# First layer of a small transformer stack: projecting the first block one sequence at a time, and the second block's projection among the first score rounds

## The chip, the cores and the metric

One Trainium2 chip, one of its cores. The metric is the device time of one launch in microseconds (us). The engines are named as in the profile: PE is TensorE's matmul, PEld its weight load, DVE is VectorE, ACT is ScalarE, POOL is GpSimd, SP is SyncE, which only issues transfers here. A q behind a name (SPq, ACTq) is that engine's sequencer, which issues DMAs.

## What is computed

The input is 16 sequences of 256 tokens with 128 channels. Four residual layers follow one another: causal attention with 16 heads of 8 channels (layer a), a mixture of 8 experts of which each token takes 2, attention without a mask with its own scaling (layer b), and the same mixture again. Cut to what matters here:

```python
x = x + attn_a(layernorm(x), wq, bq, wk, bk, wv, bv, wo, bo)   # causal, 16 heads of 8
x = x + ffn(layernorm(x), Wr, Wg, Wu, Wd)                      # top 2 of 8 experts
x = x + attn_b(layernorm(x), W_qkv, b_qkv, W_proj, b_proj)     # no mask, own scaling
x = x + ffn(layernorm(x), Wr, Wg, Wu, Wd)
```

The change is in layer a alone, in its first steps.

## The kernel before

The tokens are taken in 8 blocks of 512, that is of two sequences each; a block is held as four tiles of 128 tokens. For each block `project` computes the norms and the three projections. Its steps are: load the block; the moments (two DVE instructions for each tile, then POOL makes `rstd` and, where ScalarE is to norm, `shift`); the normed tiles `xn`; the four transposes of `xn` by PE and the copy `xnT` by ACT; k (matmul, bias on ACT, split into `hi` and `lo` by ACT and POOL); `lay` of k; q in the same way; `lay` of q; then v. `lay` spreads k or q over partitions so that every pair of heads has a row group of its own: four DMAs of 128 KB for one sequence, two from `hi` and two from `lo`, into one of four slots `ks[i]`, `qs[i]`. `project` is a generator: each `yield` gives the number of rounds until its next step and that step's load on VectorE, ScalarE and the one spare PSUM bank `mm`.

The attention itself runs in rounds. A round takes two pairs of heads of a sequence: 8 rounds make a sequence, 16 a block, 128 the layer. In round `at`, PE first computes the scores of that round with queries on the rows (`rows_scores`, tile `s<-k,q`), DVE takes their maxima (`rows_maxima`, tile `mx`), and 14 rounds later the scores are computed again, with the maxima folded in, for the exponentials on ACT. So rounds 0 to 7 read the first sequence's slots, 8 to 15 the second's, and round 16 is the first one of block 1.

All other work hangs on the rounds. `later(n, kind, steps, rank)` puts a generator on a list; `due`, called twice in each round, takes one step of every generator whose time has come, lowest rank first, as far as a budget for VectorE, ScalarE and the bank allows (rank -1 ignores the budget). Each engine takes its instructions in the order in which the Python emits them, so a matmul that waits holds back all of PE that is emitted behind it, and the same holds for each DMA queue.

Before the first round, the kernel before runs block 0's `project` for both sequences up to q, and block 1's `project` up to the transposes of its normed tiles:

```python
                second = project(1)
                next(second)
                while start() is not None:
                    pass
                later(2, work(s=0.7, bank=True), start.of, 0)
                later_constants()
...
                for i in range(2, RING):
                    later(0, FREE, prepared(i), 0)

                for _ in range(3):
                    step = next(second)
                later(*step, second, 0)
```

`prepared(i)` sets a slot's k and q tiles to zero on POOL (for slots 2 and 3) and lays rows of ones into it. In both layers `normed` (VectorE) is used for blocks 0 and 1, `normed_in_steps` (ScalarE) for later ones.

Of the kernel before, what the change touches and what calls it, by code (L numbers as in the profile page):

```python
# [41 lines left out]
F32 = mybir.dt.float32  # L42
# [4 lines left out]
ALU = mybir.AluOpType  # L47
# [16 lines left out]
NT = TB // P  # L64
# [14 lines left out]
def work(v=0.0, s=0.0, bank=False):  # L79

    return bank, v, s


FREE = work()
# [4 lines left out]
def layers(  # L89
# [21 lines left out]
    nc = tc.nc  # L111
    xt = x.flatten_outer_dims().rearrange("(n t p) d -> n p t d", t=NT, p=P)
# [49 lines left out]
    tables = ctx.enter_context(tc.tile_pool(name="tables", bufs=1))  # L162
    psum = ctx.enter_context(tc.tile_pool(name="mm", bufs=1, space=PSUM))
    x_first = blocks.tile([P, NT, P], F32, tag="xb")
    nc.sync.dma_start(out=x_first, in_=xt[0])
    queue = nc.scalar
    weights_a = attention_weights(
        wq_a, bq_a, wk_a, bk_a, wv_a, bv_a, wo_a, bo_a, 1.0 / math.sqrt(HD), "a"
# [59 lines left out]
    vs = [const.tile([P, NT, NH, 1 + HD], F32, name=f"v{i}") for i in range(3)]  # L228

    qs = [const.tile([P, NP, SEQ], F32R, name=f"q{i}") for i in range(RING)]  # L230
    ks = [const.tile([P, NP, SEQ], F32R, name=f"k{i}") for i in range(RING)]
# [3 lines left out]
    class InOrder:  # L235
# [78 lines left out]

    def moments(pool, xb, whole=False, ts=range(NT)):

        mv = pool.tile([P, NT, 2], F32, tag="mv")
        for t in ts:
            if t == NT // 2 and not whole:
                yield 1, work(0.9)  # L320
            st = pool.tile([P, nc.vector.BN_STATS_DIM], F32, tag="st", bufs=4)
            ve.bn_stats(st, xb[:, t, :])
            ve.bn_aggr(mv[:, t, :], st)
        rstd = pool.tile([P, NT], F32, tag="rstd")
        some = slice(ts[0], ts[-1] + 1)
        po.tensor_scalar_add(rstd[:, some], mv[:, some, 1], EPS)
        po.tensor_tensor(rstd[:, some], rstd[:, some], minus_half[:, some], ALU.pow)

        shift = pool.tile([P, NT], F32, tag="shift")
        if not whole:  # L330
            po.tensor_scalar_mul(shift, mv[:, :, 0], -1.0)
            po.tensor_tensor(shift, shift, rstd, ALU.mult)
        return mv, rstd, shift

    def normed_in_steps(xn, xb, rstd, shift):
        for t in range(NT):
            if t == NT // 2:
                yield 1, work(s=0.8)
            se.activation(
                xn[:, t, :], xb[:, t, :], AF.Identity,  # L340
                bias=shift[:, t : t + 1], scale=rstd[:, t : t + 1],
            )

    def normed(xn, xb, mv, rstd, ts):
        for t in ts:
            ve.tensor_scalar(
                xn[:, t, :], xb[:, t, :], mv[:, t, 0:1], rstd[:, t : t + 1],
                ALU.subtract, ALU.mult,
            )
# [463 lines left out]
    def attention(w, causal, name, mixture, ahead=None):  # L813

        with ExitStack() as own:
            pool = own.enter_context(tc.tile_pool(name=f"att_{name}", bufs=2))
# [28 lines left out]
            def project(n, b0=0, nb=2):  # L845
# [4 lines left out]
                xb, ts = xs[n], range(2 * b0, 2 * (b0 + nb))  # L850
# [3 lines left out]
                if not causal:  # L854
                    po.tensor_tensor(xb[:, ts[0] : ts[-1] + 1], xb[:, ts[0] : ts[-1] + 1], more, ALU.add)
                    yield 1, work(0.9)
                mv, rstd, shift = yield from moments(pool, xb, n < 2, ts)
                yield 3 if causal else 2, work(s=0.8)
                if causal and n == 0:
                    w["arrange"](ve)  # L860
                xn = pool.tile([P, NT, P], F32, tag="xn", bufs=1)
                if n < 2:
                    normed(xn, xb, mv, rstd, ts)
                else:
                    yield from normed_in_steps(xn, xb, rstd, shift)
                yield 2, work(s=0.6, bank=True)
                xnT = turned_block(pool, mm[0], xn, ts)

# [49 lines left out]
                for t in ts:  # L918
                    te.matmul(
                        pv[:, t, :], lhsT=xnT[:, bass.ts(t, P)], rhs=w["wv"],  # L920
                        start=True, stop=True,
# [6 lines left out]
                        :, ts[0] * NH : (ts[-1] + 1) * NH, :  # L928
                    ],
                )  # L930
                if causal and n == 0:

                    yield 1, FREE
                    yield from output_bias(w, pool, psum, name)
                while "extra" not in w:
                    yield 1, FREE
                some = xb[:, ts[0] : ts[-1] + 1, :]
# [291 lines left out]
            def later(rounds_on, kind, task, rank=1):  # L1229
                tasks.append((at + rounds_on, kind, rank, task))  # L1230

            def due(place):
                nonlocal taken
                over = at >= len(rounds)
                if place == 0:
                    taken = [0.0, 0.0]
                banks = 1
                for task in sorted((t for t in tasks if t[0] <= at), key=lambda t: (t[2], t[0])):
                    since, (bank, *times), rank, steps = task
                    more = 3.0 if over else 1.0 + 0.2 * (at - since)  # L1240
                    if rank >= 0 and (bank and not banks or any(
                        t and had and had + t > most * more
                        for t, had, most in zip(times, taken, room)
                    )):
                        continue
                    banks -= bank
                    taken = [had + t for had, t in zip(taken, times)]
                    tasks.remove(task)
                    then = next(steps, None)
                    if rank < 0 and then is not None and then[0] < 3:  # L1250

                        then = next(steps, None)
                    if then is not None:
                        later(then[0] if rank >= 0 or then[0] > 2 else 0, then[1], steps, rank)

            def fill():

                for _ in zeros():
                    yield 6, FREE

            if not causal:
                starts = [Steps(project(0, b, 1)) for b in range(2)]
                yield starts
# [6 lines left out]
            av = psum_v.tile([P, 2, SEQ], F32, tag="av")  # L1270
            ve.memset(av, 0.0)
            if causal:
                start = Steps(project(0))
                start()
                start()
                for i in range(2):
                    po.memset(ks[i].bitcast(F32), 0.0)
                start()
                for i in range(2):
                    ve.memset(qs[i].bitcast(F32), 0.0)  # L1280
                mask()
                for i in range(2):
                    for _ in prepared(i):
                        pass
                    po.memset(vs[i][:, :, :, 0], 1.0)
                po.memset(vs[2][:, :, :, 0], 1.0)
                second = project(1)
                next(second)
                while start() is not None:
                    pass  # L1290
                later(2, work(s=0.7, bank=True), start.of, 0)
                later_constants()
                later(16, FREE, fill())
                later(32, FREE, second_weights(pool, psum))
                for i in range(2, RING):
                    later(0, FREE, prepared(i), 0)

                for _ in range(3):
                    step = next(second)
                later(*step, second, 0)  # L1300
            else:
                begun, other = starts
                while not begun.ready:
                    begun()
                if not other.steps:
                    other()
                second = project(1)
                next(second)
                later(2, work(s=0.7, bank=True), begun.of, 0)
                later(0, FREE, chain(other.of, second), -1)  # L1310
            for n in range(2, NB):
                later((n - 1) * each - (9 if causal else 15), FREE, project(n), 0)
            while at < len(rounds) + lag + 4 or tasks or mixture.now:
                if at < len(rounds):
                    n, b, f, i = rounds[at]
# [3 lines left out]
                    s = rows_scores(n, b, 2 * f + i)  # L1319
# [53 lines left out]
    second = attention(weights_b, False, "b", following, mixture)  # L1373
    first, other = next(second)
# [59 lines left out]
```

## Time and profile before

| | us |
|---|---|
| median of three runs | 1261.02 (1259.92 to 1266.01) |
| the profiled execution | 1241.97 |
| its span (first to last instruction of the program) | 1239.7 |
| first score matmul (round 0) starts at | 35.27 |
| round 8 (second sequence) starts at | 47.90 |
| round 14 (first exponentials) starts at | 57.00 |
| round 16 (block 1) starts at | 62.09 |
| PE busy in the span | 1023.6 (83%) |

The starts of rounds are those of the groups `s<-k,q` on PE in the timeline, counted from the first. Times in the timeline run from the span's start. Nearly every row carries the line L245, that of the helper through which the kernel issues its instructions, so rows are told apart by their tiles: `k<-hi` is a DMA of `lay`, `xn<-xb,mv,rstd` a norm on VectorE, `xn<-xb,shift,rstd` a norm on ScalarE, `ps<-ident,xn` a transpose, `mx<-s` the maxima of a round. A bracket behind a row gives the engine's idle time ahead of it and what ended that.

### The profile page before, as it was taken

To read this page: it belongs to the slowest core of one execution; us is meant where nothing else is said; L and a number is where in the kernel's file an instruction comes from. 1 tells how busy PE (TensorE), PEld (TensorE's weight loads), DVE (VectorE), ACT (ScalarE), POOL (GpSimd) and SP (SyncE) were. 2 spreads that over 40 slices of the span, in tenths; PEclk is the share of its full clock that TensorE was granted. 3 is DMA by queue.
4 is the path that set the end of the run, shared out by engine and by line. 5 is a ranking of instruction groups with operands and counts; after the bars stand their busy time and mean duration, and the time that the engine had idled before them with its cause. 6 is when DMAs were issued, how large, how long until landed. Compare 5 with 4: busy or idle time off the path is not lost. (4 is left out here: it accounts for less than half of the span.)

```text
span 1239.7 us, 24231 instructions
## 1 busy us (share of the span) xinstructions
PE 1023.6 (83%) x8170; PEld 748.3 (60%) x8170; DVE 819.2 (66%) x2264; ACT 634.3 (51%) x1323; POOL 617.2 (50%) x687
## 2 busy tenths in 40 slices
PE   1798989878998999996577787768878888999991
PEld 0455555555776889985344444435546667799991
DVE  5666777876865766665577767667677536766662
ACT  1266666545554434453256676565746674444440
POOL 5344577555477785565221212332335675765551
PEclk9999999989999999999568899797979999999996
DMA  4334442425344698775232222222243436787866
GB/s 96 84 93 135 130 125 77 121 63 154 87 108 119 171 221 197 175 192 112 67 87 71 57 74 66 75 82 66 78 119 88 117 95 151 183 207 188 203 145 212
DMA packets 186478, 151.61 MB, mean 122 GB/s; under 512 B 16370, under 2 KB 161268, under 8 KB 186356
## 3 DMA queue, kind: packets, MB, share of 16 engines
q1 hardware_dynamic: 154754, 125.81, 36.0%
q0 software_dynamic: 26560, 18.76, 10.1%
q10 hardware_dynamic: 5042, 5.51, 1.5%
q8 instruction: 65, 1.06, 0.4%
q14 instruction: 57, 0.47, 0.1%
HBM read 82.74 MB, written 32.54 MB: 93 GB/s over the span
## 5 line engine op out<-in xcount | busy, mean ns | idle before, releaser
L245 DVE TENSOR_REDUCE mx<-s 128x6 f32<-128x768 f32 (+1 forms) x256 | 277.4, 1088 | 91.3 <-PE s L245 86.5
L245 ACT ACTIVATE p<-s 128x768 f32<-128x768 f32 (+1 forms) x256 | 234.8, 917 | 184.8 <-PE s L245 181.8
L245 POOL DMA_INDIRECT total<-y,to x156 | 244.0, 1564 | 138.9 <-ACT sg L245 80.5
L245 DVE SCALAR_TENSOR_TENSOR sg<-sg,gu 128x256 f32<-128x256 f32 x265 | 111.3, 420 | 144.5 <-ACT sg L245 108.5
L245 POOL DMA_INDIRECT rows_in<-both_rows,slots x128 | 127.5, 996 | 99.4 <-DVE both_rows L245 46.9
L245 PE MATMUL gu<-xT,w_g 128*128 128x256 f32 x530 | 162.4, 388 | 17.2 <-DVE sg L245 8.7
L245 PEld LDWEIGHTS y<-w_d,h 128*128 128x128 f32 x1248 | 165.0, 193 | 17.2 <-ACT y L245 4.8
L245 PE MATMUL y<-w_d,h 128*128 128x128 f32 x1248 | 167.4, 277 | 6.8 <-ACT y L245 3.7
L245 ACT ACTIVATE sg<-gu 128x256 f32<-128x256 f32 x265 | 101.7, 384 | 138.6 <-PE gu L245 87.1
L245 PE MATMUL gu<-xT,w_u 128*128 128x256 f32 x530 | 158.1, 380 | 0.0
L245 POOL TENSOR_SCALAR_AFFINE_SELECT p<-p 128x512 f32<-128x512 f32 x128 | 88.6, 698 | 107.6 <-ACT p L245 107.1
L245 PE MATMUL s<-k,q 62*128 62x256 f32 (+1 forms) x1024 | 136.2, 348 | 6.7 <-DVE mx L245 4.8
L245 PE MATMUL av<-p,v 128*9 128x256 f32 (+1 forms) x2048 | 134.4, 382 | 0.1
L245 PE MATMUL s<-q,k 64*128 64x256 f32 (+1 forms) x1024 | 109.4, 293 | 27.2 <-DVE mx L245 24.5
L245 PEld LDWEIGHTS s<-k,q 62*128 62x128 f32 x1024 | 83.5, 202 | 75.6 <-issue 43.2
L245 PEld LDWEIGHTS s<-q,k 64*128 64x128 f32 x1024 | 83.1, 197 | 44.2 <-DVE mx L245 33.0
L245 PEld LDWEIGHTS gu<-xT,w_u 128*128 128x128 f32 x530 | 100.8, 190 | 13.7
L245 PEld LDWEIGHTS gu<-xT,w_g 128*128 128x128 f32 x530 | 87.3, 190 | 29.5 <-DVE sg L245 10.4
L245 DVE SCALAR_TENSOR_TENSOR h<-gu,sg 128x256 f32<-128x256 f32 x233 | 98.9, 424 | 8.0
L245 ACT ACTIVATE y<-y,x_in 128x128 f32<-128x128 f32 x156 | 57.3, 368 | 78.3 <-PE y L245 74.4
L245 PEld LDWEIGHTS av<-p,v 128*9 128x9 f32 x2048 | 45.4, 93 | 70.9 <-issue 39.4
L245 POOL TENSOR_TENSOR lo<-to,hi 128x512 fp32r<-128x512 f32 (+1 forms) x25 | 31.9, 1275 | 87.3 <-ACT hi L245 87.3
(223 smaller groups left out, 1414.8 us busy)
## 6 DMA issues: line engine op xcount, KB each, us to landing
w_g<-in_L_ffn_Wg_dram SPq DMA_DIRECT2D x78, 256.0 KB
w_u<-in_L_ffn_Wu_dram SPq DMA_DIRECT2D x78, 256.0 KB
w_d<-in_L_ffn_Wd_dram SPq DMA_DIRECT2D x78, 256.0 KB
x_in<-rows_in SPq DMA_DIRECT2D x78, 130.0 KB
k<-hi SPq DMA_DIRECT2D x64, 128.0 KB
k<-lo SPq DMA_DIRECT2D x64, 128.0 KB
q<-hi SPq DMA_DIRECT2D x56, 128.0 KB
q<-lo SPq DMA_DIRECT2D x56, 128.0 KB
```

The lines of the kernel that those rows point to most:

```text
L245: return tc.keep_in_program_order(method(*args, **kwargs))
```

## The change

The first block is loaded in two halves and projected one sequence at a time, with `begun` for its first sequence and `other` for its second. The norms of all of layer a are on ScalarE (`normed_in_steps` takes the tiles `ts`). Only the first sequence is projected ahead of round 0. The second sequence's projection and, chained behind it, that of block 1 are put among the rounds with rank -1: at most two steps in a round, without the budget. The exception in `due`, by which a generator of rank -1 may take two steps at once, is now for layer b alone. The clearing of slots 2 and 3 begins at round 2.

```diff
     x_first = blocks.tile([P, NT, P], F32, tag="xb")
-    nc.sync.dma_start(out=x_first, in_=xt[0])
+    for b in range(2):
+        some = slice(2 * b, 2 * b + 2)
+        nc.sync.dma_start(out=x_first[:, some, :], in_=xt[0][:, some, :])
...
-                mv, rstd, shift = yield from moments(pool, xb, n < 2, ts)
+                mv, rstd, shift = yield from moments(pool, xb, n < 2 and not causal, ts)
                 yield 3 if causal else 2, work(s=0.8)
-                if causal and n == 0:
+                if causal and n + b0 == 0:
                     w["arrange"](ve)
                 xn = pool.tile([P, NT, P], F32, tag="xn", bufs=1)
-                if n < 2:
+                if n < 2 and not causal:
                     normed(xn, xb, mv, rstd, ts)
                 else:
-                    yield from normed_in_steps(xn, xb, rstd, shift)
+                    yield from normed_in_steps(xn, xb, rstd, shift, ts)
...
-                    if rank < 0 and then is not None and then[0] < 3:
+                    if rank < 0 and not causal and then is not None and then[0] < 3:
...
             if causal:
-                start = Steps(project(0))
-                start()
-                start()
-                for i in range(2):
-                    po.memset(ks[i].bitcast(F32), 0.0)
-                start()
+
+                begun, other = (Steps(project(0, b, 1)) for b in range(2))
+                begun()
+                po.memset(ks[0].bitcast(F32), 0.0)
                 for i in range(2):
                     ve.memset(qs[i].bitcast(F32), 0.0)
+                for _ in prepared(0):
+                    pass
                 mask()
-                for i in range(2):
-                    for _ in prepared(i):
-                        pass
-                    po.memset(vs[i][:, :, :, 0], 1.0)
-                po.memset(vs[2][:, :, :, 0], 1.0)
+                begun()
+                po.memset(ks[1].bitcast(F32), 0.0)
+                for t in vs:
+                    po.memset(t[:, :, :, 0], 1.0)
+                while not begun.ready:
+                    begun()
                 second = project(1)
                 next(second)
-                while start() is not None:
+                for _ in prepared(1):
                     pass
-                later(2, work(s=0.7, bank=True), start.of, 0)
+                later(2, work(s=0.7, bank=True), begun.of, 0)
+                later(0, FREE, chain(other.of, second), -1)
                 later_constants()
                 later(16, FREE, fill())
                 later(32, FREE, second_weights(pool, psum))
                 for i in range(2, RING):
-                    later(0, FREE, prepared(i), 0)
-
-                for _ in range(3):
-                    step = next(second)
-                later(*step, second, 0)
+                    later(2, FREE, prepared(i), 0)
```

Two smaller edits go with it: `moments` and `normed_in_steps` touch only the tiles `ts` and yield in their middle only when they hold all four; the bias of the output (`output_bias`) is computed once, by the first sequence's generator.

More of the change, by code (lines that the diff above doesn't have):

```diff
@@ L318, in moments @@
         for t in ts:
-            if t == NT // 2 and not whole:
+            if t == NT // 2 and t > ts[0] and not whole:
                 yield 1, work(0.9)
@@ L330, in moments, with normed_in_steps @@
         if not whole:
-            po.tensor_scalar_mul(shift, mv[:, :, 0], -1.0)
-            po.tensor_tensor(shift, shift, rstd, ALU.mult)
+            po.tensor_scalar_mul(shift[:, some], mv[:, some, 0], -1.0)
+            po.tensor_tensor(shift[:, some], shift[:, some], rstd[:, some], ALU.mult)
         return mv, rstd, shift
-    def normed_in_steps(xn, xb, rstd, shift):
-        for t in range(NT):
-            if t == NT // 2:
+    def normed_in_steps(xn, xb, rstd, shift, ts=range(NT)):
+        for t in ts:
+            if t == NT // 2 and t > ts[0]:
                 yield 1, work(s=0.8)
@@ L930, in project @@
                 )
-                if causal and n == 0:
+                if causal and n + b0 == 0:
                     yield 1, FREE
```

## Prediction

> **What bounds the kernel now.** I read the page first: PE is busy 1023.6 us of 1239.7, and the chain that ended last runs along PE. So what delays PE early delays the end by as much, and this change touches only the first rounds. The table of windows then shows where PE stands there.
>
> ```profile
> span 1239.7 us, 24231 instructions
> PE 1023.6 (83%) x8170; PEld 748.3 (60%) x8170; DVE 819.2 (66%) x2264; ACT 634.3 (51%) x1323; POOL 617.2 (50%) x687
> ```
> ```profile
> 20.00:30.00 10.00, 0.00 (x0) 0.00 (x0) 5.22 (x16) 0.00 (x0) 7.19 (x23) 1.00 0.97 197
> 35.30:47.90 12.60, 12.53 (x73) 7.29 (x72) 7.20 (x8) 3.85 (x7) 3.45 (x4) 1.00 0.18 47
> 57.00:62.10 5.10, 3.76 (x22) 2.12 (x22) 3.35 (x7) 2.01 (x4) 2.36 (x5) 0.52 0.37 99
> ```
>
> A row gives the window, its length, busy us of PE, PEld, DVE, ACT, POOL, the granted clock, DMA share and GB/s. PE does nothing from 20 to 30; from 35.3 on it is full. The timeline tells why it starts at 35:
>
> ```profile
> 26.99 3.55 POOL L245 MEMSET k<- 128x2048 f32 x2
> 27.07 7.61 DVE L245 TENSOR_SCALAR xn<-xb,mv,rstd 128x128 f32<-128x128 f32 x4 [1.50 <-POOL rstd L245]
> 30.48 3.55 POOL L245 MEMSET q<- 128x2048 f32 x2
> 34.25 1.08 PE L245 MATMUL ps<-ident,xn 128*128 128x128 f32 x4 [16.74 <-DVE xn L245]
> 35.27 0.79 PE L245 MATMUL s<-k,q 62*128 62x128 f32 x4
> ```
>
> Block 1's norms on DVE stand behind four POOL memsets (one takes 7.04 us), and PE, in order, has block 1's transposes ahead of round 0. Round 0's own copies had landed by 26.8 (landing records), so the norms cost 8 us and the large first projection the rest. The second loss:
>
> ```profile
> 49.70 0.60 SPq L245 DMA_DIRECT2D xb<-in_L_attn_a_x_dram  x1
> 55.19 0.29 DVE L245 BATCH_NORM_STATS2 st<-xb 128x6 f32<-128x128 f32 x1 [2.10 <-DMA xb<-in_L_attn_a_x_dram]
> 57.00 0.64 PE L245 MATMUL s<-k,q 62*128 62x128 f32 x4 [2.77 <-DVE mx L245]
> ```
>
> DVE waits for block 2, the maxima are late, PE idles 2.77 us, and the clock is at half rate (cold) from 57.2 to 67.44 (clock records). The copies are the price of what moves:
>
> ```profile
> 42.68 1.23 SPq L245 DMA_DIRECT2D k<-hi  x2
> 44.03 1.19 SPq L245 DMA_DIRECT2D k<-lo  x2
> ```
>
> The queue spends 0.62 us on each copy; landed 2.4 us after its issue when alone, 3.0 with others, 4 to 5 when SP and ACT issued together (22.7 to 26.8, 22.87 to 27.44).
>
> **The change part by part.** I add up by rounds R0, R8, R9, R14, R16, R24, since PE's order puts a wait in front of each but the last.
>
> *To R0: 19.2 instead of 35.27.* DVE clears q first (av to 1.5, two of 1.77 and gaps: 5.3), so the moments begin at 5.3 rather than 3.89. Two tiles 0.85; `rstd` and `shift` 1.95 (57.84 to 59.79): 8.2. Two ACT norms 0.87 (row 60.09), transposes, `xnT` of half size 0.38: 9.9. k's matmul 1.04 (half of 2.07), bias 0.44, `hi` 0.37: 11.8. q's matmul waits for the bank: 11.45 to 12.5, bias, `hi`: 13.3. Four copies on ACT's queue, the last issued at 15.2. Alone it lands at 17.6. Here a page speaks against the split over two queues: the Trainium skill, "DMA: Bandwidth & Descriptors", section "Issuing engines are not separate DMA queues", says that DMAs of all issuing engines run on the same 16 DMA engines and interleave. The trace agrees: with both queues at work ten copies landed between 23.49 and 29.96, 0.65 us each. Eight copies and block 1 (256 KB, two units) from 14.25 on give 20.1 instead of 17.6. The queues overlap for only half of the time, so I take 19.2. Before, k's second copy was also held 4.6 us by a semaphore whose last user was a q copy; whether it recurs the trace can't say: 0 to 3 us.
>
> *R0 to R8: 19.2 instead of 12.6.* Three cold rounds of 1.26 (36.53 - 35.27), v of one sequence 1.2, two warm rounds of 0.75 and one waiting; then the bias product. It waits for POOL: `wide` is emitted behind two memsets and the second sequence's `rstd`, whose moments wait behind maxima on DVE. That is 2.7 us of stall; ACT's norms, behind the bias copy, add 0.9. Before R8 come the second sequence's k matmul (round 7), bias and `hi` 1.3, `lo` behind POOL's addition, four SP issues 2.5, landing 2.4 to 3: PE stands 5 to 7 us. The four ones rows and the load of block 2 lie ahead on SP, long done.
>
> *R8 to R9: 7.4 instead of 2.5.* `due` takes q's matmul in round 8, after that round's scores, and `lay` of q in its second visit. So q is computed only when R8's wait is over, and R9 waits for it: scores and mask 1.0, matmul 1.0, bias and `hi` 0.8, four ACT issues 2.5, landing 2.4. ACT's queue holds nothing urgent meanwhile; DVE has no maxima to take.
>
> *R9 to R14: 9.7 instead of 6.6.* The clock is down after two waits: rounds of 1.26 again, v 1.25, the maxima's transposes 0.6, block 1's transposes and a k matmul of 1.02. Removed: the wait for block 2, which now loads at about 22, before the queue's copies.
>
> *R14 to R16: 11.7 instead of 5.1.* Block 1's k is computed in round 13, its `lay` comes in 14, q's in 15. R16 reads block 1. ACT first makes round 0's exponentials (0.81 behind 0.75 of PE), then k's `hi` (0.62): done 2.2 us after R14. Then SP has k of the first sequence, k of the second (due one round later) and only then q of the first: 12 x 0.62 = 7.5, landing 2.4. PE stands about 7.5 us. Before, q's `lo` of this sequence was issued at 48.48, 13 us ahead of its round.
>
> *R16 to R24: 20.3 instead of 18.6.* Equal work. Before, the clock was back at 67.44, 5.3 us after R16; now PE comes from 7.5 us of idleness. The Trainium skill, "TensorE: Matmul & The Clock Gate", section "HAM oscillation — how this bites in real kernels", says that idling longer than one window of 3.4 us throttles the clock, and a busy window of that length frees it. By it the third wait costs one window, some 1.5 us at the pitches 2.28 (59.81 to 62.09, cold) and 1.75 (69.87 to 71.60, warm). The trace is harsher: 2.77 us of waiting brought three windows, 10.24 us. By the page R16 to R24 would be 18.6, as before; by the row, with some of those rounds busier, 20.3. I take the row.
>
> Sum: R24 at 19.2 + 19.2 + 7.4 + 9.7 + 11.7 + 20.3 = 87.5; before it was at 80.65. That is **7 us later**. The norms' DVE time (11.8 us in 8 instructions) is freed where DVE waits anyway: nothing. The second DMA for half a block: 0.5 us of SP at the start, nothing. Layer b and everything past R24 are unchanged; PE is nearly full there, so I carry the 7 us to the end. The profiled execution took 1241.97 us (span 1239.7 and 2.3 around it), the runs 1261.02; I apply the shift to the median: 1268.
>
> **The rivals.**
>
> *A, mine, 0.56:* three waits of PE eat the earlier start and more: 1261.02 + 7 = 1268, between 1264 and 1276.
>
> *B, they only eat it, 0.34:* the copies land in 2.3 us (as at 46.42) rather than 3, R0 comes at 17.6, and the clock recovers in one window. Each of the three waits loses 0.6, R0 1.6, the clock 1.7: 5 us off, so +2, 1263. For it: lone copies took 2.3 to 2.5. Against it: twelve of them in a row took 3.0 at 52.33.
>
> *C, faster, 0.10:* the mechanism is that copies are hidden because queues run ahead of PE. If the k and q of the second sequence and of block 1 were issued as far ahead as before, R8, R9 and R16 would wait for nothing: their spans fall by about 8, 5 and 7 us, R24 comes at 67 and the time is 1248. It decides when the three waits sum to less than about 9 us, where I have 20. Against it: the matmuls that feed these copies are emitted only one to three rounds ahead.
>
> That the change doesn't do what it says is partly so: block 1's k, q and v were among the first rounds before, only its norms and transposes were not.
>
> **How the numbers follow.** About 0.5%, 6.3 us, is what a measurement of this kernel can tell from no change. A's centre lies just above it; with a possible semaphore wait (up to 3), a late landing such as block 2's 5.5 us, and more cold windows it reaches to 1276; B reaches down to 1257. The range 1257 to 1276 leaves C and the worst of A out. Faster by over 0.5% is C, 0.10; slower than 1267.3 is most of A, 0.54; between them 0.36.
>
> **What would show it.** Right: the first `s<-k,q` near 19, `xn` rows on ACT; idle brackets of 5 to 8 us on PE ahead of rounds 8, 9 and 16; `q<-hi` on SP behind eight k copies; half clock after each. Wrong: R0 later than 23, or the brackets ahead of R8, R9 and R16 together under 9 us; then C. If R24 is early but the end isn't, the loss lies past what I read.

## The result, and the profile after

The changed kernel takes 1277.95 us (median of 6 runs, 1271.93 to 1282.19), the kernel before 1263.39 (6 runs, 1259.92 to 1267.28). The ratio is 1.0116, with a 95% interval of 1.0082 to 1.0151: slower by 1.2%. A second comparison of the same two kernels, made later and with more runs, is told below; it gave 1.0063 (1.0042 to 1.0083). Slower both times, by 8 to 15 us where the forecast said 7.

The head of the page of the changed kernel. Its profiled execution took 1271.93 us.

```profile
span 1269.9 us, 24264 instructions
PE 1039.0 (82%) x8174; PEld 758.8 (60%) x8174; DVE 805.7 (63%) x2256; ACT 637.9 (50%) x1337; POOL 620.4 (49%) x698
```

PE has four matmuls more than before and 15 us more busy time, so its matmuls ran slower; about half of that, 8 us, lies behind round 24 (987.0 us of busy PE there against 978.8). DVE lost 8 instructions, ACT got 14. The moved norms are seen in ACT's timeline: two pairs of `xn`, the second one in round 6.

```profile
8.42 0.88 ACT L247 ACTIVATE xn<-x_first,shift,rstd 128x128 f32<-128x128 f32 x2 [1.90 <-POOL shift L247]
32.39 0.88 ACT L247 ACTIVATE xn<-x_first,shift,rstd 128x128 f32<-128x128 f32 x2
```

PE's timeline, rounds 0, 1, 5, 8, 9, 14, 16 and 19 (start, duration, engine, line, tiles, number of instructions, and in brackets the idle time ahead with its releaser):

```profile
20.86 0.80 PE L247 MATMUL s<-k,q 62*128 62x128 f32 x4 [7.57 <-DMA k<-ones]
22.12 0.79 PE L247 MATMUL s<-k,q 62*128 62x128 f32 x4
...
28.04 0.80 PE L247 MATMUL s<-k,q 62*128 62x128 f32 x4
...
41.54 0.80 PE L247 MATMUL s<-k,q 62*128 62x128 f32 x4 [5.53 <-DMA k<-lo]
49.18 0.80 PE L247 MATMUL s<-k,q 62*128 62x128 f32 x4 [5.45 <-DMA q<-lo]
...
61.04 0.79 PE L247 MATMUL s<-k,q 62*128 62x128 f32 x4
...
73.61 0.79 PE L247 MATMUL s<-k,q 62*128 62x128 f32 x4 [7.04 <-DMA q<-lo]
...
79.60 0.50 PE L247 MATMUL s<-k,q 62*128 62x128 f32 x4
```

The first round starts 14.4 us earlier than before (20.86 against 35.27). The bracket of round 0 names `k<-ones`, but the trace's records of when copies landed say otherwise: PE's sequencer was let go at 20.44, by the last q copy (20.41), and the 0.4 us up to 20.86 went into its further waits, which were over by then. Three more idle brackets stand ahead of rounds 8, 9 and 16: 5.53, 5.45 and 7.04 us. And every group `s<-k,q` of four score matmuls takes 0.80 us up to round 17, 0.50 only from 79.6 on. The windows of the same kernel put both losses into numbers (columns: window, length, busy us of PE, PEld, DVE, ACT and POOL, granted clock, DMA share, GB/s):

```profile
20.00:30.00 10.00, 8.52 (x40) 4.81 (x40) 5.92 (x10) 0.37 (x1) 2.44 (x4) 1.00 0.13 34
24.00:28.00 4.00, 4.00 (x20) 2.38 (x18) 2.53 (x4) 0.37 (x1) 0.00 (x0) 1.00 0.19 57
36.00:41.50 5.50, 0.01 (x1) 0.00 (x0) 0.78 (x5) 0.88 (x2) 0.72 (x1) 1.00 0.36 97
43.70:49.20 5.50, 0.05 (x3) 0.05 (x2) 0.17 (x1) 0.88 (x2) 1.40 (x2) 1.00 0.36 95
65.00:68.50 3.50, 1.57 (x16) 1.29 (x14) 2.68 (x5) 1.94 (x4) 2.22 (x3) 1.00 0.72 196
66.60:73.60 7.00, 0.00 (x0) 0.02 (x1) 2.71 (x5) 0.60 (x2) 2.77 (x3) 0.64 0.74 202
68.50:78.80 10.30, 5.19 (x40) 3.09 (x42) 2.84 (x3) 2.75 (x5) 2.15 (x3) 0.50 0.54 147
73.60:91.50 17.90, 16.37 (x158) 9.43 (x158) 8.75 (x12) 11.29 (x18) 6.15 (x9) 0.86 0.24 74
```

In 20 to 30, empty before, PE is now busy, without a gap from 24 to 28. In 36 to 41.5, 43.7 to 49.2 and 66.6 to 73.6 it stands, and no other engine is busy for half of the time: what passes is the time of copies on a queue. The clock's column must be read with care: this trace's clock records begin at 65.1 us, and a window ahead of them reads 1.00 whatever the clock was. There the duration of a known group tells the rate: 0.80 us is the slow one, as at 73.61, where the record says 0.50. The record's first stretch, 65.1 to 68.5, is at the full rate and ends in the third wait; the half rate after it lasts to 78.8.

What PE waited for is on the queues of SP and ACT (issue time, queue busy, two copies to a row). Ahead of rounds 8, 9 and 16 stand:

```profile
36.98 1.23 SPq L247 DMA_DIRECT2D k<-hi  x2
38.31 1.24 SPq L247 DMA_DIRECT2D k<-lo  x2
```
```profile
44.71 1.19 ACTq L247 DMA_DIRECT2D q<-hi  x2
46.00 1.22 ACTq L247 DMA_DIRECT2D q<-lo  x2
```
```profile
63.54 1.23 SPq L247 DMA_DIRECT2D k<-hi  x2
65.00 1.17 SPq L247 DMA_DIRECT2D k<-lo  x2
66.22 1.25 SPq L247 DMA_DIRECT2D k<-hi  x2
67.51 1.27 SPq L247 DMA_DIRECT2D k<-lo  x2
68.88 1.20 SPq L247 DMA_DIRECT2D q<-hi  x2
70.17 1.21 SPq L247 DMA_DIRECT2D q<-lo  x2
```

The last block is the third wait: twelve copies in one queue, eight of k before the first of q, 7.8 us from the start of the first issue to the end of the last, and then 2.2 us until round 16.

The rounds by which the forecast was summed, in us (the kernels "again" are the second comparison):

| | R0 | R8 | R9 | R14 | R16 | R24 |
|---|---|---|---|---|---|---|
| before | 35.3 | 47.9 | 50.4 | 57.0 | 62.1 | 80.7 |
| before, again | 35.3 | 48.7 | 51.2 | 57.8 | 62.9 | 82.0 |
| forecast | 19.2 | 38.4 | 45.8 | 55.5 | 67.2 | 87.5 |
| after | 20.9 | 41.5 | 49.2 | 61.0 | 73.6 | 91.5 |
| after, again | 20.9 | 41.4 | 49.1 | 60.9 | 73.5 | 92.0 |

The start is kept to 0.1 us in both profiles of the changed kernel; R24 is 10.8 and 10.0 us later than before.

### The profile page after: what moved, and what is told of

The parts are those of the page before. It is cut to its first block, busy times and chain, and to the rows that moved or that the text cites. A ratio compares the mean times of both kernels' runs of the same rounds, so it can differ in the third digit from the quotient of the medians.

```text
span 1269.9 us, 24264 instructions
## 1 busy us (share of the span) xinstructions
PE 1039.0 (82%) x8174; PEld 758.8 (60%) x8174; DVE 805.7 (63%) x2256; ACT 637.9 (50%) x1337; POOL 620.4 (49%) x698
## 5 line engine op out<-in xcount | busy, mean ns | idle before, releaser
L247 PE MATMUL s<-k,q 62*128 62x256 f32 (+1 forms) x1024 | 140.5, 357 | 32.2 <-DMA q<-lo 12.5
L247 PEld LDWEIGHTS s<-k,q 62*128 62x128 f32 x1024 | 86.7, 209 | 105.6 <-issue 75.9
L247 PE MATMUL av<-p,v 128*9 128x256 f32 (+1 forms) x2048 | 137.3, 390 | 0.0
L247 PEld LDWEIGHTS s<-q,k 64*128 64x128 f32 x1024 | 83.6, 198 | 41.5 <-DVE mx L247 30.4
L247 PEld LDWEIGHTS av<-p,v 128*9 128x9 f32 x2048 | 45.9, 94 | 71.2 <-issue 41.4
L247 POOL TENSOR_TENSOR lo<-to,hi 128x512 fp32r<-128x512 f32 (+1 forms) x27 | 32.2, 1193 | 83.4 <-ACT hi L247 83.2
```

The lines of the kernel that those rows point to most:

```text
L247: return tc.keep_in_program_order(method(*args, **kwargs))
```

## The experiments

Each kernel was timed beside the kernel before on the same chip. There were three groups, each on a chip of its own; the kernel before had medians of 1265.05, 1244.84 and 1244.87 us in them, so only ratios are compared across groups. The theory put to the test was that the three waits for copies eat the early start and more; its rivals were a clock that stays low, a start that doesn't reach the end, and, for the norms, that it is ScalarE and not the split by sequence that makes the start early.

### First group

**Does a delay at the start reach the end?** The kernel before, with 36 memsets on DVE ahead of block 1's norms:

```diff
-                for _ in range(3):
+                for k in range(3):
+                    if k == 1:
+                        for _ in range(36):
+                            ve.memset(av, 0.0)
                     step = next(second)
```

> The kernel before with 36 more clearings of a tile on DVE (0.48 us each) ahead of block 1's norms, so that round 0 starts about 11 us later, at 46 instead of 35.3; nothing else is changed. Theory (a delay of the first rounds goes to the end one for one, and the changed kernel's 14.6 us are its 11 us at round 24 and scatter): round 24 near 91.5, and the time 9 to 13 us above the kernel before. Rival 1 (later stages take a delay up): under 5 us. Rival 2 (later stages add to it, by the throttle's windows or by something in the changed kernel's later stages): with rival 2 in general 15 us or more; if only the changed kernel's later stages add, 11 us here against 14.6 there.

Measured: 1279.89 us, 1.0141 (1.0106 to 1.0176). R0 came at 50.8 instead of 35.3, R24 at 96.4 instead of 80.7. The row for one memset is 0.48 us long, but they follow at 0.67, and the delay was 15.5 us where 11 were expected:

```profile
45.02 0.48 DVE L245 MEMSET av<- 128x512 f32 x1 [0.18 <-DVE av L245]
45.69 0.48 DVE L245 MEMSET av<- 128x512 f32 x1 [0.18 <-DVE av L245]
```

The delay is 15.5 us at R0, 15.7 at R24 and 14.8 in the time (1279.89 - 1265.05; 0.0141 x 1265 = 17.8 by the ratio, its interval 13.4 to 22.3). The rest of the kernel does not absorb it. So R24 can be read for the end, as far as a delay of this kind goes.

**The waits ahead of rounds 9 and 16, through the order of the steps.** The changed kernel, with two steps at a time for layer a again, so that q is projected before its copies' rounds come:

```diff
-                    if rank < 0 and not causal and then is not None and then[0] < 3:
+                    if rank < 0 and then is not None and then[0] < 3:
```

> The changed kernel with one edit undone: in due a generator of rank -1 may again take two steps at once when the next is due in under three rounds. Theory (three waits for copies in front of rounds 8, 9 and 16, at half clock): k and q of the second sequence are then laid in rounds 6 and 7 and block 1's in rounds 10 and 11, so the waits of 5.5 us ahead of round 9 and of 7.0 us ahead of round 16 go, the one ahead of round 8 stays at 4 to 7. Round 24 comes near 78 instead of 91.5, and the time falls by 11 to 16 us against the changed kernel, to about that of the kernel before (within 5 us). Rival (the loss lies in the half clock of the first rounds and in later stages, the waits are only its sign): round 24 comes no earlier than 86 and the time stays within 5 us of the changed kernel.

Measured: 1269.83 us, 1.0053 (1.0016 to 1.0089); R24 at 83.2, 8 us earlier than after. PE's rows of rounds 8, 11, 12 and 16, and the copies of k ahead of round 8:

```profile
44.32 0.79 PE L247 MATMUL s<-k,q 62*128 62x128 f32 x4 [4.83 <-DMA k<-lo]
...
52.15 0.80 PE L247 MATMUL s<-k,q 62*128 62x128 f32 x4
...
57.98 0.79 PE L247 MATMUL s<-k,q 62*128 62x128 f32 x4
...
64.38 0.80 PE L247 MATMUL s<-k,q 62*128 62x128 f32 x4
```
```profile
37.89 3.79 SPq L247 DMA_DIRECT2D k<-lo  x2
```

The waits ahead of 9 and 16 are gone, and from R8 to R16 the kernel takes 20.1 us instead of 32.1: 12.0 less, nearly the 12.5 of the two brackets. Block 1's matmuls are still there, at the slow rate (5.8 us from round 11 to 12, for its q and v). It was expected to gain more at R24, and two things took about 4 us back. R8 comes 2.8 us later, with a wait of 4.83: the row of two `k<-lo` copies is 3.79 us long and not 1.2, because the second was held 2.6 us by a semaphore that a q copy had used last (SP's waits: `DMA q<-hi`, 2.6), and q had now been put before it. And R16 to R24 takes 18.9 instead of 17.9. So the order of steps is worth 8 us of R24.

**All copies of the first block ahead of round 0.** The changed kernel, with the second sequence's k and q projected before round 0 and block 1 left for round 9:

```diff
                 while not begun.ready:
                     begun()
+                for _ in range(8):
+                    other()
...
-                later(0, FREE, chain(other.of, second), -1)
+                later(9, FREE, chain(other.of, second), -1)
```

> The changed kernel, but the second sequence too is projected up to its laid q ahead of round 0 (still one after the other); block 1's steps come in the same rounds as in the changed kernel, so its wait ahead of round 16 stays. Theory: PE was idle from 13.3 to 20.9 anyway, so round 0 moves back by only 1 to 4 us; the waits ahead of rounds 8 and 9 (5.5 and 5.5 us) and the stall for the output's bias go partly; round 16 keeps its wait of about 7 us; round 24 near 80 to 84; 8 to 12 us faster than the changed kernel. Rival (round 0 is set by the copies' bandwidth: 1 MB more ahead of it pushes it to 27 or later): round 24 at 88 or later, under 4 us faster.

Measured: 1267.05 us, 1.0024 (1.0001 to 1.0046). R0 at 21.7, only 0.8 us later than in the changed kernel, although four projections instead of two stand ahead of it on PE; R8 at 35.7 and R9 at 38.1 without a wait for a copy. Then:

```profile
61.63 0.80 PE L247 MATMUL s<-k,q 62*128 62x128 f32 x4 [7.33 <-DMA q<-lo]
```

The wait for block 1 stays. R24 comes at 79.2, 12.3 us earlier than after. The brackets of rounds 8 and 9 had 10.98; the second sequence's transposes and k and q matmuls, 2.8 us of PE, went into the idle time ahead of round 0 as well. The norms are as in the changed kernel, so its loss lies for the most part in the waits: the copies ahead of round 0 hide, the same copies behind it do not.

**The clock's share.** The changed kernel with matmuls that nobody reads, ahead of rounds 0, 8, 9 and 16, in the time in which PE stands:

```diff
+                    if causal and at in (0, 8, 9, 16):
+                        idle = mm[0].tile([P, TB], F32, tag="mm")
+                        for _ in range({0: 40, 8: 36, 9: 34, 16: 50}[at]):
+                            te.matmul(
+                                idle[:, 0 : 2 * P].rearrange("p (c m) -> p c m", m=P),
+                                lhsT=ident_h, rhs=mask_q, start=True, stop=True,
+                            )
                     s = rows_scores(n, b, 2 * f + i)
```

> The changed kernel with matmuls that nobody reads (bf16, 128 x 256) put on PE ahead of rounds 0, 8, 9 and 16, 40, 36, 34 and 50 of them, about as long as PE idles there. It adds work and takes none away. Theory (the term that I mis-sized is the clock: it was at half rate from round 0 to round 17): the clock is up, score rounds go at 0.75 to 1.0 instead of 1.26 us, round 16 starts near 64 to 66 instead of 73.6, round 24 near 82 instead of 91.5, and the time falls by 6 to 10 us although the waits for the copies remain. Rival (the clock is a mere companion, the chain of copies alone paces the start): round 16 within 2 us of 73.6, no change or slower.

Measured: 1270.86 us, 1.0063 (1.0040 to 1.0086); R16 at 69.2 and R24 at 85.3, 6.2 us earlier than after although work was added. PE's rows:

```profile
13.95 5.91 PE L247 MATMUL idle<-mask_q,ident_h 128*128 128x256 bf16 x40 [0.66 <-ACT to L247]
20.75 0.49 PE L247 MATMUL s<-k,q 62*128 62x128 f32 x4 [0.89 <-DMA k<-ones]
21.50 0.50 PE L247 MATMUL s<-k,q 62*128 62x128 f32 x4
...
29.54 0.80 PE L247 MATMUL s<-k,q 62*128 62x128 f32 x4
...
69.21 0.50 PE L247 MATMUL s<-k,q 62*128 62x128 f32 x4 [0.59 <-DMA q<-lo]
```

Rounds 0 to 5 run 0.75 us apart instead of 1.26, and R0 comes at the same time as after: it waits for its copy either way. But the clock falls again ahead of round 6, and the matmuls don't keep it up to round 16; R16 was expected at 64 to 66. So the low clock is a loss of its own, worth at least 6 us of R24, beside the waits. In the time this is not clear: the changed kernel itself had 1.0116 in one comparison and 1.0063 in the other.

### Second group

**Block 1 early too.** As the third experiment, with block 1 let in from round 2:

```diff
-                later(9, FREE, chain(other.of, second), -1)
+                later(2, FREE, chain(other.of, second), -1)
```

> The kernel of e5 (both sequences of block 0 laid ahead of round 0) with block 1's steps beginning in round 2 instead of 9, so that its copies are issued some 7 rounds ahead of round 16. Theory: of e5 only the wait of 7.3 us ahead of round 16 goes; round 0 stays near 21.7, round 16 comes near 53 to 56 instead of 61.6, round 24 near 71 to 74 instead of 79.2, and the time is 4 to 8 us below e5's, so 2 to 7 us below the kernel before. Rival (block 1's steps among the first rounds cost as much there as the wait did: bank, DVE and clock): round 24 at 77 or later, time within 2 us of e5.

Measured: 1235.50 us, 0.9921 (0.9892 to 0.9950): faster than the kernel before. The last of the three waits shrinks to

```profile
54.91 0.79 PE L247 MATMUL s<-k,q 62*128 62x128 f32 x4 [1.79 <-DMA k<-hi]
```

and R24 is at 73.6, 17.9 us ahead of the changed kernel's 91.5; the three brackets had 18.0. That these agree so well is partly chance, since 1.79 us of the third wait stay and the second sequence's 2.8 us of PE work are gone from between the rounds.

**The same with 20 unread matmuls between the two projections.**

```diff
+                idle = mm[0].tile([P, TB], F32, tag="mm")
+                for _ in range(20):
+                    te.matmul(
+                        idle[:, 0 : 2 * P].rearrange("p (c m) -> p c m", m=P),
+                        lhsT=ident_h, rhs=mask_q, start=True, stop=True,
+                    )
                 for _ in range(8):
                     other()
```

> The kernel of e6 with 20 matmuls that nobody reads (bf16, 128 x 256) on PE between the two sequences' projections, where PE would idle for 4 us. Theory (the half clock of the first rounds costs 0.3 to 0.5 us a round): the clock comes up before round 0 for one or more windows, round 8 comes 2 to 4 us earlier than in e6, the time is 1 to 4 us lower. Rival (rounds are then bound by the maxima on DVE at about 1 us, and the clock falls again): under 1 us.

Measured: 1231.69 us, 0.9905 (0.9876 to 0.9934); R0 at 20.6 and R24 at 70.9, 2.7 us earlier. The intervals overlap, so the gain is shown in the rounds only. Rounds 0 to 2 run at the fast rate; from 27.1 to 46.5 us the score groups are at 0.80 again.

**The norms alone.** The kernel before, with ScalarE making the norms of layer a's first two blocks (`shift` is made for them too, as in the changed kernel, and block 1's transposes stay ahead of round 0):

```diff
-                if n < 2:
+                if n < 2 and not causal:
                     normed(xn, xb, mv, rstd, ts)
...
-                for _ in range(3):
+                for _ in range(4):
                     step = next(second)
```

> The kernel before with one part of the change alone: norms of blocks 0 and 1 of layer a by ScalarE instead of VectorE (in layer b too those blocks get a shift on POOL that nobody reads). Block 1's transposes stay ahead of round 0. Theory: VectorE's norms of block 1 stood 7 us behind POOL's memsets; on ScalarE four take 1.75 us from 27.6, so round 0 comes near 30 instead of 35.3, block 0's copies too come about 1 us earlier, round 24 near 75 to 77 and the time 3 to 6 us below the kernel before. Rival (something else, the copies or the constants, holds round 0 to 33 or later): under 2 us.

Measured: 1233.21 us, 0.9922 (0.9894 to 0.9950). The timeline of ACT, POOL and PE:

```profile
25.61 3.55 POOL L245 MEMSET k<- 128x2048 f32 x2
25.71 1.65 ACT L245 ACTIVATE xn<-xb,shift,rstd 128x128 f32<-128x128 f32 x4 [8.79 <-POOL shift L245]
```
```profile
27.98 0.79 PE L245 MATMUL s<-k,q 62*128 62x128 f32 x4
```

Four norms take 1.65 us on ACT beside the same memsets behind which DVE took 7.61 in the kernel before. R0 comes at 28.0 instead of 35.3, R24 at 74.3 instead of 80.7 and 82.0. This part of the change alone is a gain of 0.8% (0.5 to 1.1%).

**Block 1 later, without the split.** The kernel before with ScalarE's norms (the lines of the last experiment, not shown again), one step at a time, slots 2 and 3 cleared from round 2 on, and block 1 among the rounds, from round 2 on; block 0 is still projected whole:

```diff
-                    if rank < 0 and then is not None and then[0] < 3:
+                    if rank < 0 and not causal and then is not None and then[0] < 3:
...
-                    later(0, FREE, prepared(i), 0)
-
-                for _ in range(3):
-                    step = next(second)
-                later(*step, second, 0)
+                    later(2, FREE, prepared(i), 0)
+
+                later(2, FREE, second, -1)
```

> The kernel before with block 0 projected whole as it was, norms of blocks 0 and 1 of layer a on ScalarE, and block 1's steps (all but its load) not ahead of round 0 but from round 2 on with rank -1, one step a visit (in layer b too blocks 0 and 1 get a shift on POOL that nobody reads). It tells the one-sequence-at-a-time part from the rest. Theory: round 0 is held by the copies of the first sequence, which share the queues with the second's: round 0 near 25 to 28, round 16 near 54 to 60, round 24 near 73 to 77, time 3 to 8 us below the kernel before. Rival (splitting block 0 is what brings the early start, without it nothing is left): within 2 us of the kernel before.

Measured: 1232.51 us, 0.9911 (0.9888 to 0.9934). R0 is at 23.1, 2.2 us later than with the split, R8 at 38.6, R9 at 44.0, R16 at 54.4, R24 at 73.0:

```profile
23.09 0.80 PE L245 MATMUL s<-k,q 62*128 62x128 f32 x4 [7.47 <-DMA q<-hi]
...
54.44 0.80 PE L245 MATMUL s<-k,q 62*128 62x128 f32 x4
```

PE waits for no copy after round 0 up to 80 us. Against this kernel, projecting by sequence buys 2.2 us at round 0 (20.9), and the changed kernel pays 11.0 for them ahead of rounds 8 and 9.

### Third group

**The same with a warm start**, 40 unread matmuls ahead of round 0:

```diff
+                idle = mm[0].tile([P, TB], F32, tag="mm")
+                for _ in range(40):
+                    te.matmul(
+                        idle[:, 0 : 2 * P].rearrange("p (c m) -> p c m", m=P),
+                        lhsT=ident_h, rhs=mask_q, start=True, stop=True,
+                    )
                 later(2, work(s=0.7, bank=True), start.of, 0)
```

> The kernel of e9 with 40 matmuls that nobody reads (bf16, 128 x 256) on PE behind block 0's projection, where PE idles 7.5 us until the first copies have landed. Theory (half clock costs 0.3 to 0.5 us in each early round): rounds 0 to 2 go at 0.8 to 1.0 instead of 1.27 us, later rounds keep the warm clock of e9 and the time is 0 to 3 us below e9's 0.9911 of the kernel before, the lowest of all. Rival (the maxima on DVE and the bias product bound the rounds): no difference to e9.

Measured: 1232.50 us, 0.9895 (0.9856 to 0.9934), the lowest ratio of all.

```profile
23.31 0.49 PE L245 MATMUL s<-k,q 62*128 62x128 f32 x4
24.06 0.50 PE L245 MATMUL s<-k,q 62*128 62x128 f32 x4
```

The first rounds run at 0.75, but R24 comes at 71.9, only 1.1 us earlier. PE now waits for maxima on DVE (3.6 us in six waits up to 80 us, where the version without the warm start has 1.3), and the clock falls early: rounds 7 and 8 are at 0.80 (35.40, 40.25), where that version has 0.50. The five versions of the last two groups that beat the kernel before (0.9895 to 0.9922) can't be told apart by their intervals; all five beat both kernels.

**Is the third wait the queue's issue time?** The changed kernel, with the second sequence's copies of block 1 two rounds later, so that fewer of them stand ahead of the first's q:

```diff
-                        later(max(b, free_at - at), FREE, task, 0)
+                        later(max(3 * b if causal and n == 1 else b, free_at - at), FREE, task, 0)
```

> The changed kernel, with the copies of the second sequence of block 1 two rounds later, so that on SP's queue the first sequence's q follows directly on its k (8 copies instead of 12 ahead of round 16). Theory (the wait ahead of round 16 is the issue time of the queue, 0.63 us a copy, and then one landing): round 16 starts 2.5 us earlier, near 71.1 instead of 73.6, its wait is 4.5 instead of 7.0, and the time 2 to 3 us below the changed kernel's 1.0116 of the kernel before. Rival (the wait is for landing under load, not for the issue): round 16 within 1 us of 73.6.

Measured: 1250.52 us, 1.0033 (1.0010 to 1.0057).

```profile
70.97 0.80 PE L247 MATMUL s<-k,q 62*128 62x128 f32 x4 [4.92 <-DMA rows_in<-blank]
```

R16 came at 71.0 and the wait fell from 7.04 to 4.92 us: four copies by 0.63 are 2.5. The releaser in the bracket is another copy of the same queue, issued at 68.76 behind the last `q<-lo`; as at round 0, the bracket need not name the copy that mattered. R16 came 2.6 us earlier (73.61 - 70.97), where 2.5 were expected: within 0.1 us the queue's issue time is in the wait one for one.

**The two kernels again**, the changed one and, as a control, the kernel before against itself:

> The changed kernel, once more, on the same chip as the others of this call, for a second profile and for its ratio: theory as for before_again, rounds 0, 8, 16 and 24 at 20.9, 41.5, 73.6 and 91.5 within 0.5 us, ratio 1.009 to 1.015. Rival (its start scatters, by the lane that a copy waits for or by the clock's windows): more than 2 us of difference at round 24.

> The kernel before, once more, for a second profile of it: its first profiled execution took 1241.97 us where its runs on that chip had a median of 1265. Theory (chips differ, the start doesn't): rounds 0, 8, 16 and 24 at 35.3, 47.9, 62.1 and 80.7 within 0.5 us, and a ratio of 1; what differs from profile to profile lies behind round 64. Rival (the first rounds scatter too): more than 2 us of difference at round 24, and then the 11 us at round 24 are not a firm figure.

Measured: 1253.07 us against 1244.87, 1.0063 (1.0042 to 1.0083), and for the control 1246.24, 1.0024 (0.9999 to 1.0049). The control shows that a ratio of this kernel may be off by a quarter of a per cent for no reason in the code. So 1.0116 and 1.0063 are both taken as measurements of a change of about 0.9%.

### What the shift of round 24 says of the time

Before stands at 81.3 (mean of its two profiles, 80.65 and 81.97), after at 91.8 (mean of 91.50 and 92.02).

| kernel | R24 minus 81.3, us | as a share of 1250 us | measured ratio |
|---|---|---|---|
| delay of 36 memsets | +15.0 | +1.20% | 1.0141 |
| after (both profiles) | +10.4 | +0.83% | 1.0116 and 1.0063 |
| block 1's copies later | +8.1 | +0.65% | 1.0033 |
| unread matmuls | +4.0 | +0.32% | 1.0063 |
| two steps at a time | +1.9 | +0.15% | 1.0053 |
| first block ahead of round 0 | -2.1 | -0.17% | 1.0024 |
| norms alone | -7.0 | -0.56% | 0.9922 |
| block 1 from round 2 too | -7.7 | -0.62% | 0.9921 |
| block 1 later, no split | -8.4 | -0.67% | 0.9911 |
| the same, warm | -9.4 | -0.76% | 0.9895 |
| split, early, warm | -10.4 | -0.84% | 0.9905 |

The two columns agree within about 0.4%. What is left over goes with the comparison more than with the kernel: the four of the first group, where the kernel before took 1265 us, lie 0.2 to 0.4% above their shift, and all of the two others 0.1 to 0.3% below it. Such a leftover is nearly half of the change's own 0.9%, so a difference between two of these kernels of less than about 0.4% can't be read from their times alone. The first measurement of the change, with 1263 us before, lies 0.33% above and the second 0.2% below.

## Why the prediction was right or wrong

**The path.** Right: the added delay of PE in the first rounds reached the end (15.5 us at R0 gave 14.8 of time), and the rows ahead of rounds 8, 9 and 16 are waits for copies, of 5.53, 5.45 and 7.04 us where the text said "idle brackets of 5 to 8 us on PE ahead of rounds 8, 9 and 16". Taking away those of 9 and 16, those of 8 and 9, and nearly all three brought R24 forward by 8, 12 and 18 us. The direction was right too: rivals B and C have fallen, the first because R24 was 10 us late and not 2, the second because the waits summed to 18 us and the rival needed fewer than 9.

**The step that failed: the clock.** The working had "Three cold rounds of 1.26" and then "two warm rounds of 0.75" in R0 to R8, and went on to price block 1's k matmul at the warm "1.02". In the kernel before the rate had risen so, between round 2 (0.77 at 39.51) and round 3 (0.50 at 41.44). Here it did not: every score group up to round 17 took 0.80 us. The rate was up only from 65.1 to 68.5, mostly inside the third wait, and then for good from 78.8 on. The second profile of the changed kernel has clock records from 35.8 on and says the same: half rate from 39.2 to 63.1 and from 69.9 to 80.2, full rate from 35.8 to 39.2, in the first wait, and from 63.1 to 69.9. By the terms:

| span | forecast | after | what made the difference |
|---|---|---|---|
| to R0 | 19.2 | 20.9 | the last q copy issued 1.0 later, landing 0.2 longer, 0.45 from landing to matmul |
| R0 to R8 | 19.2 | 20.7 | rounds 3 to 7 at the slow rate, a shorter stall for the bias product |
| R8 to R9 | 7.4 | 7.6 | - |
| R9 to R14 | 9.7 | 11.9 | k matmul 2.07, not 1.02; two waits for ACT of 0.46 and 0.68 |
| R14 to R16 | 11.7 | 12.6 | twelve issues began 2.5 us after R14 and took 7.8, not 2.2 and 7.5 |
| R16 to R24 | 20.3 | 17.9 | the clock was up 5.2 us after R16 |

The sums differ by 4.0 us; the last row took 2.4 back, so the others were too small by 6.4 together. By an estimate from the rounds' pitches the clock's part is at least 2.5 of it, the largest: 1.5 in R0 to R8 (three rounds at 1.26 instead of 0.75) and 1.05 for k. Beside it stand 1.7 at R0, 1.1 for two waits for ACT that the sum did not have, and 0.9 for the twelve copies.

For the third wait I had taken the harsh row (10.24 us of half clock after a wait of 2.77). It came as the row has it: 10.3 us of half clock, 68.5 to 78.8. But 5.1 us of them passed while PE stood, so the clock was back 5.2 us after R16, as it was 5.3 us after R16 in the kernel before, and the 1.7 us that I added for it did not come.

Nor is a wait of that length needed, as I had read it. In the second profile of the kernel before the group of four score matmuls is at 0.80 already at 53.05; the wait at the place of the 2.77 comes only after it and lasts 0.93:

```profile
50.89 0.38 PE L245 MATMUL ps<-ident,parts 128*32 128x128 f32 x2 [1.38 <-DVE parts L245]
51.20 0.49 PE L245 MATMUL s<-k,q 62*128 62x128 f32 x4
...
53.05 0.80 PE L245 MATMUL s<-k,q 62*128 62x128 f32 x4
...
57.85 0.79 PE L245 MATMUL s<-k,q 62*128 62x128 f32 x4 [0.93 <-DVE mx L245]
```

So the clock can fall without the wait that I took for the cause; a wait of 1.38 us stands ahead of it here.

A rule of the Trainium skill, "TensorE: Matmul & The Clock Gate", section "What's actually happening", says that the array is back at full rate after one busy window of about 3.4 us. (That section states it, and not the one on oscillation, which the forecast named for it.) The trace disagrees: PE was busy 4.00 of 4.00 us in 24 to 28, worked without a break from 20.86 to 29.3, which holds a whole window wherever the windows begin, and was still at the slow rate; in the kernel with two steps at a time it was so from 50.15 to 65 with gaps below 0.8 us. By the rule the rounds from 28 on would be 0.75 apart. In the kernel before, with the norms alone and with block 1 later the rate did rise after 5 to 8 us of work. What in the work decides is not settled: neither its length nor the presence of whole-block projections sorts all the traces.

**Round 0.** That copies of both queues slow one another was right: the last two q copies were issued at 15.63 and 16.23 and landed at 19.94 and 20.41 (the landing records), 4.3 and 4.2 us later, while both queues had copies under way. The forecast's 19.2 had 4.0 us for it, behind an issue at 15.2. So the landing was nearly right, and the miss lies in the chain ahead of it: q's matmul began at 12.07 and not at 11.45, the last issue came 1.0 us late, and 0.45 us from the landing to the first matmul were not counted. The wait for a semaphore of k's second copy, priced at 0 to 3 us, did not come here (issues at 12.48 and 13.16); it came with two steps at a time, as 2.6 us ahead of round 8.

**The bias product.** PE waited for it as said (it stands for 1.30 us up to 30.68, on POOL's `wide`), where I had 2.7.

**What remains.** The forecast lies 9.95 us below the median of 1277.95. The runs of the kernel before next to it were 2.4 us above those that I started from; the rounds make 3.4 (10.4 instead of 7); the remaining 4.2 us are not in the first rounds. The second comparison has the same pair 7.8 us apart (0.0063 x 1245), below the 10.0 of R24 in it, so this rest is not the same from one comparison to the next. Behind R24 the profiles scatter by more than it: from there to the end of the span the changed kernel took 1178.4 and 1165.0 us, the kernel before 1159.0 and 1161.5, and the kernel with the delay of 36 memsets 1174.9. The cause of the rest stays open.

**Where the gain went.** 14.4 us of earlier start went into 18.0 of waits. The rest of R24's 10 us, some 6 to 7, goes with the slow rate: the unread matmuls gave 6.2 back. The change puts together a part that is good by itself (norms on ScalarE, 0.9922), one that did no harm beside it (block 1 off the path to round 0 too, 0.9911, which the intervals do not tell from 0.9922), and one that sends copies just ahead of their use.

## What to carry to other kernels

Before starting rounds earlier, list for each later round when its inputs are issued: the copies that stood behind a slow start for free have to be counted one by one, at 0.62 us of queue and 2.3 us of landing, and a projection taken one round ahead of its use wasn't hidden here. Norms that lie blocked behind another engine's memsets are worth moving to a free engine alone, before anything is restructured around them. Price short rounds at the slow rate unless the trace shows them at the fast one in the same place, and try unread matmuls in the idle time as a test of what the clock is worth.

## What of the hardware was not expected

- DVE and POOL. Four norms on DVE lasted 7.61 us beside POOL's memsets (3.55 us each) and four norms on ACT beside the same memsets 1.65. DVE's own memsets were not held: in the changed kernel DVE cleared q at 1.88 and 4.02, 1.76 us each, the first beside POOL's memset at 1.51 (1.79), the second not. So in these rows it is not the engine alone that decides whether DVE is held.
- The clock stayed at the slow rate through 8.4 us of unbroken rounds (20.86 to 29.3), and in the kernel with unread matmuls it was up 2.9 us after the first of them (13.95; its clock record begins at 16.8).
- Half clock came in stretches of the same length after waits of different length: 10.24 us (57.2 to 67.44) after a wait of 2.77 in the kernel before, 10.3 (68.5 to 78.8) in and after one of 7.04 in the changed kernel.
- A copy can be held by another queue's copy through a semaphore that both use: 2.6 us in the kernel with two steps at a time, at 38.5.
- A row of DVE memsets of one tile, 0.48 us each, follows itself at 0.67: 0.18 us pass between two of them, each waiting for the one before.
- The same kernel before took 1265.05 us on one chip and 1244.84 and 1244.87 on two others, 1.6% apart. Whether the chip or the time of the measurement makes it was not separated.
